# A GNN layer in f32 on one core: where the first batch's residual is loaded

## The chip, the cores and the metric

The kernel runs on one core of a Trainium2 chip. The metric is the device time of one execution in microseconds (us). Before the change the median of three runs is 2159.79 us (2157.69 to 2161.91).

## What is computed

One layer of a gated graph network over 32 graphs (called batches here) of 512 nodes with 256 features, all in float32. The reference, cut to what matters:

```python
h = relu(layernorm(x))                                   # (32, 512, 256)
xc = transpose(h)                                        # channels first
c = relu(bn1(conv1d(xc, conv1_w)))                       # 1 tap
c = bn2(conv1d(c, conv2_w, pad=8))                       # 17 taps
x_conv = transpose(relu(c + xc))
s = h @ w_se.T + b_se                                    # 3 features
A = exp(-squared_distances(s)) * adj                     # (512, 512) for each batch
x_nmp = A @ relu(h @ w_msg.T + b_msg)
gi = concat([x_conv, x_nmp]) @ w_ih.T + b_ih             # 512 -> 3*256
gh = h @ w_hh.T + b_hh                                   # 256 -> 3*256
r = sigmoid(gi_r + gh_r); z = sigmoid(gi_z + gh_z)
n = tanh(gi_n + r * gh_n)
out = x + (1 - z) * n + z * h                            # the last "x +" is the residual
```

## The kernel before

Everything is kept with features on the 128 partitions and the 512 nodes of a batch along the free dimension; 256 features are two tiles, counted by `o` or `d`. The work runs as five streams: `rows` and `begins` (normalise, transpose, first convolution), `graphs` (messages, distances, the masked kernel and its product), `conv` (the 17 taps, as 25 products for each group of 4 batches, on transformed operands) and `gates` (the gated update, batch by batch).

**What sets the order.** The streams are Python generators. A planner written out in the kernel (the loop at L1106) keeps a clock of its own, `now`, advanced by an estimate for every matmul, and estimates of when VectorE (DVE) and ScalarE (ACT) are free. It always lets the stream go on that is furthest behind its share. So the order of each engine's instructions is settled when the program is built. A DMA issue moves none of these clocks: where a load stands in the program changes only the queue of the engine that issues it. Nearly all loads are issued by SyncE (SP), in program order; SP stands still at a load whose buffer is still being read, and all loads behind it wait too.

**The stretch around the change.** At the 25th product of the first group, `late_pools` (L686) opens the pool for the second half of the work and issues the gates' weights, `whh` (768 KB) and `wih` (1536 KB), on SP. This lets the stream `gates` begin: `all_gates` (L1058) waits for `late`, loads the residual of batch 0, and then runs `gates(b)` for each batch. `gates(b)` (L861) first loads `hTb` (512 KB, the normalised rows of its batch) and two tiles `xnb` (256 KB each, the graph's product), unless that was done ahead.

**The residual.** `load_res(b, o)` (L776) loads one half of a batch of `x` into a tile `res` of 128 x 512, of which the pool has three. `blocks` (L768) does it in four DMAs, one for each 32 rows. Each takes `x` in blocks of 32 x 32, laid out so that a later block transpose needs no other step; a piece that is contiguous in HBM is 32 floats, 128 B, so a DMA of 64 KB has 512 pieces. Batch 0's two halves are the eight DMAs of this case. For every later batch `store` issues the load of a half just when the half of the batch before has been stored (L928).

**Who reads it.** For each half `o`, `gates` sums four products in PSUM: `ps_r`, `ps_h`, `ps_z` and `ps_n`. Then `mix`, `mix_next`, `mix_last` and `leave` follow, each queued with `later` until the planner's clock has come to it. `leave` (L911) transposes the result block by block, adds it to `res` on DVE and queues `store`.

**The masks.** `Graphs.ask` (L253) loads 128 rows of the adjacency matrix into `m_sb` (256 KB, three buffers). Batches 0 to 7 take them row by row, and TensorE (PE) turns them with four transposes (L132, called from `masked`, L741); batches from 8 on take them in blocks of 32 x 32, in four DMAs. Each mask is asked for when the one three before it has been used.

Of the kernel before, what the change touches and what calls it, by code (L numbers as in the profile page):

```python
# [44 lines left out]
def kernel(  # L45
# [31 lines left out]
    ND = D // P  # L77
# [46 lines left out]
    def matmul(ps, lhsT, rhs, **more):  # L124
        nonlocal now
        now += max(0.22, elements(ps) / 600.0)
        nc.tensor.matmul(ps, lhsT, rhs, **more)  # L127
# [16 lines left out]
    def later(t, f):  # L144
        LATER.append((t, f))
        LATER.sort(key=lambda e: e[0])

    def settle():
        while LATER:
            LATER.pop(0)[1]()  # L150
# [29 lines left out]
    def load_gates(b):  # L180
        if b >= B or b in HB:
            return
        HB[b] = late.tile([P, ND, N], F32, name="hTb", bufs=2)
        nc.sync.dma_start(HB[b], HD[b])

    def load_sums(b, d):
        if b < B and (b, d) not in XN:
            XN[b, d] = late.tile([P, N], F32, name="xnb", bufs=2)
            nc.sync.dma_start(XN[b, d], ND_[b, d])
# [578 lines left out]
    def blocks(t, rows, o):  # L768
        for g in range(P // 32):
            at = o * P + 32 * g  # L770
            nc.sync.dma_start(
                t[32 * g : 32 * g + 32, :].rearrange("i (k j) -> i k j", j=32),
                rows[:, :, at : at + 32],
            )

    def load_res(b, o):  # L776
        if b < B and (b, o) not in XR:
            XR[b, o] = late.tile([P, N], F32, name="res", bufs=3)
            blocks(XR[b, o], XB[b], o)
# [81 lines left out]
    def gates(b):  # L861

        load_gates(b)
        load_sums(b, 0)
        load_sums(b, 1)
        hT = HB[b]
        parts = []
        x_in = []

        def cols(o, g):  # L870
            return slice(g * D + o * P, g * D + (o + 1) * P)

        def products(ps, o, g, first, last, of, then=None):


            sources = ((whh, 0), (wih, 0), (wih, ND))
            for k in range(first, last):
                w, at = sources[k]
                for i in range(ND):
                    matmul(  # L880
                        ps, w[:, at + i, cols(o, g)], hT[:, i, :] if k == 0 else x_in[2 * k - 2 + i],
                        start=(k == of[0] and i == 0), stop=(k == of[1] and i == ND - 1),
                    )
                if k == last - 1 and then is not None:
                    then()
                yield now

        def residual():
            xconv = XC.pop(b)[:, :, :N]
            dve.tensor_tensor(xconv, xconv, hT, op=ALU.add)  # L890
            yield dve.free + 0.3
            act.activation(xconv, xconv, AF.Relu)
            x_in.extend([xconv[:, i, :] for i in range(ND)] + [XN[b, d] for d in range(ND)])

        def mix_next(r, z, o, s):
            act.activation(
                r[:, s], r[:, s], AF.Tanh,
                bias=vec[:, _COL["b_ih"] + 2 * ND + o : _COL["b_ih"] + 2 * ND + o + 1],
            )
            later(act.free + 0.3, lambda: mix_last(r, z, o, s))  # L900

        def mix_last(r, z, o, s):
            if s.start == 0:
                parts.append(late.tile([P, N], F32, name="o_sb"))
            t = parts[-1]
            dve.tensor_tensor(t[:, s], hT[:, o, s], r[:, s], op=ALU.subtract)
            dve.tensor_tensor(t[:, s], z[:, s], t[:, s], op=ALU.mult)
            dve.tensor_tensor(r[:, s], r[:, s], t[:, s], op=ALU.add)
            later(dve.free, lambda: leave(r, t, o, s))

        def leave(r, t, o, s):  # L911

            dve.transpose(t[:, s], r[:, s])
            y = XR[b, o]
            dve.tensor_tensor(y[:, s], t[:, s], y[:, s], op=ALU.add)
            later(dve.free + 0.4, lambda: store(y, o, s))

        def store(y, o, s):
            for g in range(P // 32):
                at = slice(32 * g, 32 * g + 32)  # L920
                queue = nc.gpsimd if s.stop - s.start == N else nc.scalar if g % 2 else nc.sync
                queue.dma_start(  # L922
                    OB[b][:, s.start // 32 : s.stop // 32, o * P + 32 * g : o * P + 32 * g + 32],
                    y[at, s].rearrange("i (k j) -> i k j", j=32),
                )
            if s.stop == N:
                del XR[b, o]
                load_res(b + 1, o)  # L928

        for o in range(ND):  # L930
            r = z = None

            def reset():
                nonlocal r
                settle()
                r = late.tile([P, N], F32, name="r", bufs=2)
                act.activation(r, ps_r, AF.Sigmoid, bias=brz[:, o : o + 1])

            def reset_hidden():
                dve.scalar_tensor_tensor(  # L940
                    r, ps_h, vec[:, _COL["b_hh"] + 2 * ND + o : _COL["b_hh"] + 2 * ND + o + 1], r,
                    op0=ALU.add, op1=ALU.mult,
                )

            def update():
                nonlocal z
                z = late.tile([P, N], F32, name="z")
                act.activation(z, ps_z, AF.Sigmoid, bias=brz[:, ND + o : ND + o + 1])

            def mix(s=slice(0, N)):  # L950
                dve.tensor_tensor(r[:, s], ps_n[:, s], r[:, s], op=ALU.add)
                later(dve.free + 0.3, lambda r=r, z=z, o=o: mix_next(r, z, o, s))
                if o == ND - 1:
                    load_sums(b + 1, 0)
                    load_sums(b + 1, 1)

            ps_r = acc.tile([P, N], F32, name="ps_acc")
            if o == 0:
                yield lambda: b in evacuated
                yield evacuated[b]  # L960
                yield from residual()
                yield from products(ps_r, o, 0, 0, 1, (0, 2))
                yield act.free + LAG
            else:
                yield from products(ps_r, o, 0, 0, 1, (0, 2))
            yield from products(ps_r, o, 0, 1, 3, (0, 2), reset)
            ps_h = acc.tile([P, N], F32, name="ps_acc")
            yield from products(ps_h, o, 2, 0, 1, (0, 0), reset_hidden)
            ps_z = acc.tile([P, N], F32, name="ps_acc")
            yield from products(ps_z, o, 1, 0, 3, (0, 2), update)  # L970
            if o == 0:
                load_gates(b + 1)
            ps_n = acc.tile([P, N], F32, name="ps_acc")
            if b < B - 1 or o < ND - 1:
                yield from products(ps_n, o, 2, 1, 3, (1, 2), mix)
                continue

            for h in range(2):
                s = slice(h * N // 2, (h + 1) * N // 2)
                if h > 0:  # L980
                    ps_n = acc.tile([P, N], F32, name="ps_acc")
                for j in range(2 * ND):
                    matmul(
                        ps_n[:, s], wih[:, j, cols(o, 2)], x_in[j][:, s],
                        start=(j == 0), stop=(j == 2 * ND - 1),
                    )
                mix(s)
                yield now
            settle()
        gated.add(b)  # L990
# [66 lines left out]

    def all_gates():  # L1058
        yield lambda: late is not None
        for o in range(ND):  # L1060
            load_res(0, o)
        for b in range(B):
            yield from gates(b)

# [6 lines left out]
        "graphs": (all_graphs(), 49.0, 0.0),  # L1071
        "conv": (convolution(), 66.0, 0.0),
        "gates": (all_gates(), 125.0, 1.25),
    }
    clock = {name: at for name, (_, _, at) in streams.items()}
# [102 lines left out]
```

## Time and profile before

| What | us |
| --- | --- |
| median of three runs | 2159.79 |
| the profiled execution | 2163.09 |
| its span, first instruction to last | 2161.0 |
| PE busy in it | 2100.2 |
| DVE busy | 1523.7 |
| ACT busy | 763.7 |
| POOL (GpSimd) busy | 296.8 |

The span is what the profile's rows are measured in; the profiled execution has about 2 us around it. A few of its rows recur below. For the group `res<-in_x_dram` the list of DMA issues has 256 issues of 64 KB, with a median of 4.3 us from issue to landing. The masks stand there as 32 issues of 256 KB (3.6 us) and 384 of 64 KB (2.6 us), `hTb` as 32 issues of 512 KB (6.0 us). SP's queue, q1, moves 282.95 MB, and its packets take 48.3% of the 16 DMA engines' span.

How to read the lines: an instruction stands as line, engine, operation, `out<-in`, shape and count. In a timeline the first two numbers are start and duration, and square brackets hold how long the engine had been idle before it and what ended that. In a view of waits the three numbers are the total, how often, and the longest. L118, L127 and L132 are helpers that issue nearly all work of DVE and ACT, of matmuls and of transposes, so the tiles' names tell more than the line. PEld is PE's loading of weights, which overlaps its matmuls. An engine name with a q (SPq) is the engine's queue of issues.

### The profile page before, as it was taken

What the parts mean: (1) busy time and instruction counts of PE and PEld (TensorE: products, weight loads), DVE (VectorE), ACT (ScalarE), POOL (GpSimd) and SP (SyncE); (2) the same over time, 40 slices, a digit from 0 to 9 for tenths busy, and PEclk for the clock granted to TensorE, in tenths of its full rate; (3) what the DMA queues carried; (4) which work ended last, traced back from release to release, by engine and by line L of the source; (5) the groups of instructions that cost most, each with busy time, mean ns of one, the idle gap of its engine ahead of it and who ended that gap; (6) DMA issues with size and microseconds to landing.
All of it is one profiled execution on the core that took longest, in us unless ns stands there. A gap on an engine that the chain in (4) does not pass through costs nothing.

```text
span 2161.0 us, 26532 instructions
## 1 busy us (share of the span) xinstructions
PE 2100.2 (97%) x9200; PEld 1303.0 (60%) x9200; DVE 1523.7 (71%) x2818; ACT 763.7 (35%) x1277; POOL 296.8 (14%) x445
## 2 busy tenths in 40 slices
PE   7998899999999999999999999999999999999998
PEld 4876566566565666556665666556665566665443
DVE  6887588676777778668875777767777677776333
ACT  5635422424324342334424243243522325222311
POOL 1101112111111111111111111101111010011111
PEclk9999899999999999999999999999999999999999
DMA  7446566766666576756767656666676564554331
GB/s 269 164 156 217 169 195 176 235 173 181 169 201 176 168 194 183 206 165 173 191 181 212 184 160 194 189 174 189 180 183 161 151 161 138 142 169 90 71 73 34
DMA packets 539461, 367.11 MB, mean 170 GB/s; under 512 B 455232, under 2 KB 472000, under 8 KB 538688
## 3 DMA queue, kind: packets, MB, share of 16 engines
q1 hardware_dynamic: 511392, 282.95, 48.3%
q0 software_dynamic: 23248, 69.23, 10.1%
q10 hardware_dynamic: 4688, 13.24, 1.6%
q8 instruction: 73, 1.20, 0.2%
q14 instruction: 60, 0.49, 0.1%
HBM read 282.74 MB, written 82.58 MB: 169 GB/s over the span
## 4 chain that ended last, share of the span: by engine, by line
PE 83%; ACT 1%; DVE 1%; issue 0%; DVEq 0%; ACTq 0%
PE ps_acc L127 44%; PE ps_g L127 17%; PE ps_c L127 14%; PE ps_b L127 7%; PE ps_b L733 1%; PE ps_g L132 1%; ACT at L118 0%; DVE xconv L118 0%; ACT xconv L118 0%; ACT L118 0%; DVE r L118 0%; DVE o_sb L118 0%; PE ps_g L733 0%; DVE msg L118 0%; DVE res L118 0%
## 5 line engine op out<-in xcount | busy, mean ns | idle before, releaser
L127 PE MATMUL ps_acc<-xconv,wih 128*128 128x512 f32 (+1 forms) x772 | 362.5, 592 | 5.2 <-ACT xconv L118 5.2
L127 PE MATMUL ps_acc<-xnb,wih 128*128 128x512 f32 (+1 forms) x772 | 362.7, 592 | 0.0
L127 PE MATMUL ps_acc<-hTb,whh 128*128 128x512 f32 x768 | 355.6, 593 | 0.1
L127 PE MATMUL ps_c<-xd,w 128*128 128x116 f32 x2800 | 346.2, 277 | 4.4 <-DVE z L118 4.4
L127 PEld LDWEIGHTS ps_c<-xd,w 128*128 128x128 f32 x2800 | 332.0, 194 | 7.6 <-DVE z L118 4.8
L922 POOL DMA_DIRECT2D out_dram<-res x252 | 164.8, 660 | 942.3 <-DVE res L118 843.4
L118 DVE TENSOR_TENSOR r<-ps_acc,r 128x512 f32<-128x512 f32 (+1 forms) x65 | 44.4, 684 | 313.3 <-PE ps_acc L127 313.2
L127 PEld LDWEIGHTS ps_acc<-xnb,wih 128*128 128x128 f32 x772 | 141.9, 189 | 165.0 <-issue 163.4
L127 PEld LDWEIGHTS ps_acc<-xconv,wih 128*128 128x128 f32 x772 | 141.4, 190 | 157.2 <-issue 145.6
L127 PE MATMUL ps_g<-at,msg 128*128 128x512 f32 x512 | 229.5, 599 | 2.5 <-DVE at L118 2.5
L127 PEld LDWEIGHTS ps_acc<-hTb,whh 128*128 128x128 f32 x768 | 141.7, 190 | 148.1 <-issue 143.8
L127 PEld LDWEIGHTS ps_b<-x,w 128*128 128x128 f32 x1400 | 182.8, 192 | 71.1 <-issue 55.8
L118 ACT ACTIVATE mid<-ps_b 128x232 f32<-128x232 f32 x175 | 63.9, 365 | 370.7 <-PE ps_b L127 331.7
L127 PE MATMUL ps_b<-x,w 128*128 128x116 f32 x1400 | 184.3, 275 | 5.3 <-ACT at L118 5.3
L127 PEld LDWEIGHTS ps_g<-at,msg 128*128 128x128 f32 x512 | 97.1, 192 | 119.9 <-issue 113.7
L118 DVE SCALAR_TENSOR_TENSOR x<-x,x 128x480 f32<-128x480 f32 (+1 forms) x184 | 144.1, 783 | 3.0
L118 DVE TENSOR_TENSOR x<-x 128x240 f32<-128x240 f32 (+1 forms) x320 | 134.4, 462 | 0.5
L127 PE MATMUL ps_g<-wmsg,hTg 128*128 128x259 f32 x496 | 125.1, 384 | 0.7 <-ACT hT L118 0.7
L118 ACT ACTIVATE z<-ps_acc,brz 128x512 f32<-128x512 f32 x64 | 44.0, 687 | 220.5 <-PE ps_acc L127 220.3
L127 PE MATMUL ps_g<-hT,w 128*128 128x512 f32 x256 | 119.4, 610 | 1.2 <-ACT at L118 1.2
L127 PEld LDWEIGHTS ps_g<-wmsg,hTg 128*128 128x128 f32 x496 | 93.0, 191 | 44.4 <-issue 32.5
L118 DVE TENSOR_TENSOR xd<-x 128x480 f32<-128x480 f32 x175 | 113.2, 649 | 3.3 <-PE ps_c L127 3.3
(109 smaller groups left out, 2488.5 us busy)
## 6 DMA issues: line engine op xcount, KB each, us to landing
w<-wd SPq DMA_DIRECT2D x150, 768.0 KB, 5.8
m_sb<-in_adj_dram SPq DMA_DIRECT2D x384, 64.0 KB, 2.6
hd<-hT POOLq DMA_DIRECT2D x32, 512.0 KB, 5.7
res<-in_x_dram SPq DMA_DIRECT2D x256, 64.0 KB, 4.3
hTb<-hd SPq DMA_DIRECT2D x32, 512.0 KB, 6.0
xnb<-nd SPq DMA_DIRECT2D x64, 256.0 KB, 3.1
out_dram<-res POOLq DMA_DIRECT2D x252, 64.0 KB, 3.2
hTg<-hd SPq DMA_DIRECT2D x31, 512.0 KB, 4.4
```

Source lines behind the costliest of these rows:

```text
L118: getattr(self.engine, name)(*tiles, **more)
L127: nc.tensor.matmul(ps, lhsT, rhs, **more)
L132: nc.tensor.transpose(ps, a, ident)
L733: nc.tensor.matmul(pss[c], gr.left[k, :], gr.right[k, :], start=True, stop=True, tile_position=(32 * c, 0),)
L922: queue.dma_start(OB[b][:, s.start // 32 : s.stop // 32, o * P + 32 * g : o * P + 32 * g + 32], y[at, s].rearrange("i (k j) -> i k j", j=32),)
```

## The change

The eight loads of batch 0's residual are taken out of `all_gates`, where they stood ahead of `gates(0)` and so right behind the gates' weights. They now stand inside `gates(0)`, after the products into `ps_z` of the first half and behind the load of `hTb` for batch 1. Later batches are as before.

```diff
@@ gates(b), in the loop over the halves o
             yield from products(ps_z, o, 1, 0, 3, (0, 2), update)
             if o == 0:
                 load_gates(b + 1)
+                for k in range(ND if b == 0 else 0):
+                    load_res(0, k)
             ps_n = acc.tile([P, N], F32, name="ps_acc")
             if b < B - 1 or o < ND - 1:
                 yield from products(ps_n, o, 2, 1, 3, (1, 2), mix)
@@ all_gates()
         yield lambda: late is not None
-        for o in range(ND):
-            load_res(0, o)
         for b in range(B):
             yield from gates(b)
```

## The prediction

> **What bounds the kernel now.** I read the totals and slices first, then TensorE's waits, then the stretch that holds the longest of them. The page:
>
> ```profile
> span 2161.0 us, 26532 instructions
> PE 2100.2 (97%) x9200; PEld 1303.0 (60%) x9200; DVE 1523.7 (71%) x2818; ACT 763.7 (35%) x1277; POOL 296.8 (14%) x445
> ```
>
> TensorE (PE) is busy for 97% of the span. Its instructions run in one written order, so the time is its work plus its gaps, 60.8 us in all. The changed DMAs compute nothing, so they matter only through a gap. The view of waits for PE names the gaps:
>
> ```profile
> PE ps_g L132 <- DMA m_sb<-in_adj_dram: 13.5, 1, 13.5
> PE ps_g L132 <- ACT x_sb L118: 9.3, 1, 9.3
> PE ps_b L127 <- ACT at L118: 5.3, 6, 1.6
> ```
>
> The longest is one single wait of 13.5 us, for an adjacency mask from HBM. The second is the kernel's start. The timeline shows where the first lies, and SP's queue beside it:
>
> ```profile
> 204.52 0.33 SPq L470 DMA_DIRECT2D w<-wd  x1
> 204.90 10.41 SPq L771 DMA_DIRECT2D res<-in_x_dram  x8
> 215.36 0.49 SPq L184 DMA_DIRECT2D hTb<-hd  x1
> 215.94 0.85 SPq L189 DMA_DIRECT2D xnb<-nd  x2
> 216.88 0.38 SPq L173 DMA_DIRECT2D hT<-hd  x1
> 217.36 7.55 SPq L262 DMA_DIRECT2D m_sb<-in_adj_dram  x4
> ...
> 223.46 1.09 PE L132 MATMUL ps_g<-ident,m_sb 128*128 128x128 f32 x4 [13.50 <-DMA m_sb<-in_adj_dram]
> ```
>
> The eight `res` issues that the change moves stand right ahead of that mask: SP spends 10.41 us on them. The mask (the last of batch 3) is issued at 217.36 and lands 6.0 us later, at about 223.3; PE goes on at 223.46. Windows of that stretch tell what SP is held by (columns: time, busy us of PE, PEld, DVE, ACT, POOL, then the granted clock, DMA share, GB/s):
>
> ```profile
> 202.00:213.00 11.00, 7.47 (x44) 4.58 (x36) 6.84 (x8) 6.02 (x13) 0.00 (x0) 1.00 1.03 422
> 212.90:216.70 3.80, 0.00 (x0) 0.00 (x0) 2.66 (x3) 2.31 (x3) 0.00 (x0) 0.67 1.39 165
> 217.00:223.00 6.00, 0.00 (x0) 0.00 (x0) 0.00 (x0) 3.11 (x3) 0.00 (x0) 0.50 0.97 341
> ```
>
> The DMA engines are full from 202 to 223. First come the weights `whh` and `wih` (768 and 1536 KB) and three `w` at 422 GB/s, and SP's 10.41 us is mostly back pressure from them (one `res` issue took 4.83 us, the median one 0.49). From 212.9 to 216.7 the rate is 165 GB/s: there the profile counts 4256 packets, 4231 of them under 512 B, and the eight `res` loads are 8 x 512 = 4096 pieces of 128 B. So the mask waits for a backlog on the DMA engines, and not only for SP. That matters for the sum: the gain isn't 10.41.
>
> **The change, part by part.**
>
> *Removed from 204.90: eight DMAs.* In the shared backlog `res` holds 3.8 us. Without it `hTb` follows the weights at 212.9. Behind it come `xnb`, `xnb`, `hT` and the mask: 512 + 256 + 256 + 512 + 256 KB = 1.835 MB. SP reaches them early: issues of about 0.5 us from 204.9 put `hT` at 206.4. Its buffer was last read by the row product of 204.33, which ends at 207.94. The mask reuses a buffer that PE reads in the eight transposes from 207.78 to 208.82, so it is issued by about 209, well before 212.9. The wait for those bytes is then pure transfer. Before, they took from 216.7 to 223.3, 6.6 us, because SP fed them one at a time into emptying queues. At the 422 GB/s that the row shows for a backlog they take 4.35 us, with some 0.6 us to land about 4.95. So the gain is 3.8 us if they go no faster than before, and 3.8 + 1.65 = 5.45 us if they run at the backlog's rate. These are my two ends. I take 4.9, nearer to the second, since everything is queued before the engines get to it; 2 KB pieces (`xnb`, mask) are the reason not to take it all. The mask lands at about 218.4, and PE's wait is 8.6 us.
>
> The Trainium skill speaks against this size. "DMA: Bandwidth & Descriptors", section Specifications, puts the fabric ceiling at 435 GB/s, by which the 0.524 MB of `res` would be worth 1.2 us and the gain about 1.2 to 2.9. The same table says that pieces under 512 B fall short of line rate, and the row at 165 GB/s shows that here: 3.8 us measured decides.
>
> *The clock.* PE's granted clock falls about 4.2 us after PE stops (1.00 until 214.2) and comes back only at 231.2:
>
> ```profile
> 214.20:223.40 9.20, 0.00 (x0) 0.00 (x0) 1.36 (x3) 5.72 (x5) 0.00 (x0) 0.50 1.10 285
> 223.40:231.20 7.80, 6.96 (x11) 3.22 (x12) 1.82 (x2) 0.00 (x0) 0.00 (x0) 0.50 0.15 43
> ```
>
> A wait of 8.6 us still lets it fall, so the half clock after the restart (7.8 us, costing 3.9) stays. The shorter one that the page shows, after a 2.2 us wait at 298.6, held 3.4 us at half (mean 0.51 from 299.5 to 303). When the clock comes back may differ between executions by some 2.4 us of half clock: plus or minus 1.2 us; I take 0.
>
> *Does the gain last?* DVE, ACT and SP wait for PE after the restart: DVE sat idle 10.3 us before 236.7 and ACT 11.9 us before 232.05, and PE has no other wait for a DMA in the whole trace. The order on PE, DVE, ACT and POOL stays as it is, since the planner's clock doesn't count DMA issues. So all shifts together; I carry the full 4.9.
>
> *Added after `load_gates(1)`: the same eight DMAs.* In the old times, `hTb` for batch 1 is issued at 269.39, and SP's next instruction starts 7 us later:
>
> ```profile
> 268.99 0.37 SPq L262 DMA_DIRECT2D m_sb<-in_adj_dram  x1
> 269.39 0.43 SPq L184 DMA_DIRECT2D hTb<-hd  x1
> 276.81 3.00 SPq L470 DMA_DIRECT2D w<-wd  x2
> ...
> 280.56 0.69 DVE L118 TENSOR_TENSOR res<-o_sb,res 128x512 f32<-128x512 f32 x1
> ```
>
> Eight issues at 0.49 are 3.9 us, 269.8 to 273.7: they fit ahead of the 276.81 with 3.1 us left. The packets come after `hTb`, which landed at 275.3 (5.9 us). The first four loads are 1.9 us of packets, so they land at about 277.8; the add that reads them runs at 280.56: 2.8 us of cover. The other four land at about 279.7 and are read at 332.16. The moved packets may hold up the `w` of 276.81 by up to 3.8 us, from 280.1 to 283.9; the sum that reads it is the `w` group at 287.17 by my count. POOL only stores the result of the add. I cost this part at 0, with a low bound of 0 (nothing is removed here). The high bound takes the first `res` loads' longest landing, 10.0 us: the fourth, issued near 271.3, would land at 281.3, 0.8 us late. If the cover goes, DVE stands at the add, and `xd`, the mask's product `at` and `n` behind it (281.17 to 282.34) are late for PE, microsecond for microsecond.
>
> **The sum.** -4.9 + 0 + 0 = -4.9 us: the span goes from 2161.0 to 2156.1. The profiled execution took 2163.09, 3.3 above the median of the runs, 2159.79; the forecast is 2159.8 - 4.9 = **2154.9 us**, from 2153.1 to 2157.3 with the clock's 1.2 us on each side of 3.8 and 5.45.
>
> **Rivals.**
>
> *The mask is hardly earlier (2158.6).* The bytes count and not the pieces: 0.524 MB at 422 GB/s is 1.2 us. Or SP is still held, by `hT`'s buffer for one. For it: SP's issues were held by the full queues, and these stay full until 212.9. Against it: 4231 small packets in 3.8 us with almost nothing else moving.
>
> *Slower: `res` comes late to the add at 280.56.* For it: DVE runs in order, TensorE's next products wait for it, and the cover is 2.8 us after a stretch in which stores of `w` and `hTb` share the engines. The gap is paid in full and costs 1.7 more when the clock halves for 3.4 us, as at 299.5. It eats the gain when the loads land 3.2 us late, at 283.8. With 8 us it gives 8 + 1.7 - 4.9 = +4.8: 2164.6. Against it: that is a landing 17 us after its issue, where the longest seen, in the worst backlog, is 10.0.
>
> *The wait goes altogether (2142.4).* If the mask overtook the weights there would be no 13.5 us and no half clock: -17.4. Against it: one queue in order, full until 212.9. The change not doing what it says is excluded: issue order on SP is the order in the program, and no load of `res` remains early.
>
> **How the numbers follow.** Forecast 0.78, hardly earlier 0.12, late `res` 0.08, wait gone 0.02. About 0.2%, 4.3 us, is what a measurement can tell. The forecast's own range crosses that bound (2155.5): I give 0.60 of its 0.78 to the side below it, as 4.9 lies above 4.3. Faster is 0.60 + 0.02 = 0.62, same 0.18 + 0.12 = 0.30, slower 0.08. The range is 2151.5 to 2159.0: the first case with the 2 us or so that the runs scatter, and most of the second.
>
> **What would show it.** In the changed profile the mask's wait is 8 to 9.5 us, `res` is gone from the stretch before it and the DMA rate there stays above 300 GB/s; `res` is issued right after the second `hTb`, and the add doesn't wait for a DMA. A wait of over 11 us refutes the backlog's arithmetic, a DVE wait for `res` the cover, and a new PE gap after 230 the claim that the gain lasts.

## The result, and the profile after

The changed kernel is faster, and by more than what its runs scatter. The first comparison gave 2153.61 us (median of 4 runs, 2152.67 to 2154.48) against 2159.96 us, a ratio of 0.9971 with a 95% interval of 0.9954 to 0.9988. With more runs of both it is 2154.11 us against 2160.77 us, ratio 0.9971, interval 0.9961 to 0.9981: 6.3 us less, between 4.1 and 8.4. The forecast was 2154.9 us.

The waits of TensorE in the changed kernel (total, times, longest), with the kernel's start now ahead of the mask:

```profile
PE ps_g L132 <- ACT x_sb L118: 9.2, 1, 9.2
PE ps_g L132 <- DMA m_sb<-in_adj_dram: 8.6, 1, 8.6
```

The mask's wait went from 13.5 to 8.6 us, as forecast. SP's queue in the same stretch, and PE's restart:

```profile
200.85 0.49 SPq L693 DMA_DIRECT2D wih<-in_w_ih_dram  x1
203.27 0.33 SPq L470 DMA_DIRECT2D w<-wd  x1
203.65 0.42 SPq L184 DMA_DIRECT2D hTb<-hd  x1
204.16 0.86 SPq L189 DMA_DIRECT2D xnb<-nd  x2
205.11 0.38 SPq L173 DMA_DIRECT2D hT<-hd  x1
207.15 11.61 SPq L262 DMA_DIRECT2D m_sb<-in_adj_dram  x4
...
217.31 1.08 PE L132 MATMUL ps_g<-ident,m_sb 128*128 128x128 f32 x4 [8.61 <-DMA m_sb<-in_adj_dram]
```

The first mask is issued at 207.15, 10.2 us earlier than before, but it takes 10.0 us to land and not 6.0: the engines are still busy with the weights. The windows show that they now stay busy right through (time, busy us of PE, PEld, DVE, ACT, POOL, granted clock, DMA share, GB/s):

```profile
201.00:211.30 10.30, 7.21 (x40) 4.58 (x36) 6.41 (x7) 6.02 (x13) 0.00 (x0) 0.94 1.03 426
211.30:217.20 5.90, 0.00 (x0) 0.00 (x0) 2.99 (x4) 4.07 (x4) 0.00 (x0) 0.50 1.03 397
217.30:223.70 6.40, 5.60 (x10) 2.63 (x11) 1.82 (x2) 1.56 (x2) 0.00 (x0) 0.50 0.23 66
```

There is no stretch at 165 GB/s any more. The half clock after the restart lasts 6.3 us here, where it was 7.8.

The eight loads in their new place (SP), and the add that needs the first four (DVE):

```profile
262.79 0.43 SPq L184 DMA_DIRECT2D hTb<-hd  x1
263.26 8.44 SPq L771 DMA_DIRECT2D res<-in_x_dram  x8
271.87 1.09 SPq L470 DMA_DIRECT2D w<-wd  x2
...
273.69 0.69 DVE L118 TENSOR_TENSOR res<-o_sb,res 128x512 f32<-128x512 f32 x1
```

No bracket stands behind the add: it didn't wait. The fourth load was issued at 265.29 and took 6.7 us, so it landed at 272.0, with 1.7 us of cover.

**Why the two profiled spans differ by more.** They are 2161.0 and 2150.6 us, 10.4 apart. The distance between like instructions in the two traces grows in steps. It is 1.3 us already at the transposes before the wait (209.30 and 208.04), where the change has not acted yet. The wait adds 4.9, which makes 6.15 at the restart. The earlier return of the clock adds 0.7 by the next common wait (298.64 and 291.77). Two steps of 1.6 us follow, and there the clocks differ, here after the wait for `z` near 333, before and after:

```profile
333.60:337.10 3.50, 3.50 (x18) 3.50 (x19) 0.35 (x1) 1.56 (x2) 2.16 (x4) 0.51 0.72 157
```

```profile
326.50:330.00 3.50, 3.50 (x23) 2.81 (x24) 1.42 (x4) 1.62 (x2) 2.30 (x5) 1.00 0.65 131
```

After the same kind of wait (2.2 and 2.1 us) TensorE ran at half clock for 3.4 us in the one execution and at full clock in the other. The second step is such a stretch at 746.6 that has no match at 737.9. But a second profile of the changed kernel has it (738.7, clock 0.50). So 4.9 of the 10.4 us are the wait, and the rest is how long and how often the clock was halved, which differs between executions of one and the same program.

### The profile page after: what moved, and what is told of

Read it like the earlier page. It is cut to its first block, busy times and chain, and to the rows that moved or that the text cites. A ratio compares the mean times of both kernels' runs of the same rounds, so it can differ in the third digit from the quotient of the medians.

```text
span 2150.6 us, 26534 instructions
## 1 busy us (share of the span) xinstructions
PE 2092.6 (97%) x9200; PEld 1297.0 (60%) x9200; DVE 1522.8 (71%) x2818; ACT 762.9 (35%) x1277; POOL 295.9 (14%) x445
## 3 DMA queue, kind: packets, MB, share of 16 engines
q0 software_dynamic: 23248, 69.23, 10.2%
## 4 chain that ended last, share of the span: by engine, by line
PE 83%; ACT 1%; DVE 1%; issue 0%; DVEq 0%; ACTq 0%
PE ps_acc L127 44%; PE ps_g L127 17%; PE ps_c L127 13%; PE ps_b L127 7%; PE ps_b L733 1%; PE ps_g L132 1%; ACT at L118 0%; DVE xconv L118 0%; ACT xconv L118 0%; ACT L118 0%; DVE r L118 0%; DVE o_sb L118 0%; PE ps_g L733 0%; DVE msg L118 0%; DVE res L118 0%
```

## The experiments

In two profiles each, the mask's wait was 13.5 and 13.9 us in the kernel before, 8.6 and 9.3 us in the changed one. So two profiles of one kernel lie 0.4 and 0.7 us apart; a smaller difference says nothing. The question is what of those eight DMAs delays the mask: SP's time, the pieces, the bytes or their number.

**Half of them back.**

```diff
         yield lambda: late is not None
+        load_res(0, 0)
```

> The changed kernel, with the first half of batch 0's residual (four of the eight loads) back in the old place. In the changed kernel TensorE waits 8.6 us for the last mask of batch 3, in the kernel before 13.5 us. If the pieces of res take time on the DMA engines in line ahead of the mask, half of them put back half: about 1.9 us of packets and some refilling, a wait of 10.5 to 11.1 us. If SP's issue time is what counts, the wait follows SP: the first four issues took 6.4 of the 10.4 us, so 8.6 + 4.9 x 0.61 = 11.6 us. The two lie close; the run is mainly a check that the effect comes in doses.

The wait was 11.6 us: the effect comes in doses. It falls on the number that went by SP's time, but the 11.1 of the pieces lies within the scatter. SP's queue in that run:

```profile
203.23 6.48 SPq L771 DMA_DIRECT2D res<-in_x_dram  x4
209.75 2.35 SPq L184 DMA_DIRECT2D hTb<-hd  x1
```

The four issues alone took 6.48 us (the third 4.95), and in SP's waits of the stretch none of them, nor `hTb`, waits for a landing. So `hTb` was issued at 209.75, where the changed kernel issues it at 203.65. The number alone, by the rule found below, would have let `hTb` go by 205.4, but the mask itself not before 213.1; it went at 213.62.

**Issued by another queue.**

```diff
-            blocks(XR[b, o], XB[b], o)
+            blocks(XR[b, o], XB[b], o, nc.gpsimd if b == 0 else nc.sync)
```

> The kernel before, with the eight loads of batch 0's residual in the old place but issued by GpSimd's queue and not by SP's. Theory (work on the shared DMA engines): SP is free early, but the same 4096 pieces still run on the same engines before the mask, and the wait stays at 12 to 13.5 us. Rival (SP's queue held by the issues): SP goes straight on to hTb and the mask, and the wait falls to 8.6 us as in the changed kernel.

The wait grew to 16.2 us. SP was as free as in the changed kernel (queue of that run):

```profile
202.22 0.33 SPq L470 DMA_DIRECT2D w<-wd  x1
202.60 0.43 SPq L184 DMA_DIRECT2D hTb<-hd  x1
203.12 1.16 SPq L189 DMA_DIRECT2D xnb<-nd  x2
204.37 0.46 SPq L173 DMA_DIRECT2D hT<-hd  x1
206.10 10.94 SPq L262 DMA_DIRECT2D m_sb<-in_adj_dram  x3
```

and the shared engines had become slower, 238 GB/s where the changed kernel had 426 and then 397 (a window of that run):

```profile
206.00:218.00 12.00, 1.16 (x9) 0.69 (x7) 7.21 (x8) 6.66 (x8) 1.56 (x3) 0.62 1.02 238
```

16.2 us is above both numbers that were expected. So freeing SP while the same rows run beside the weights doesn't help, and SP's time can't be all. It is no clean price for the pieces, though: on GpSimd's queue the profile counts 261 packets for these 0.54 MB, not some 4096, so they go out in another form there.

**Large pieces, eight DMAs.** Batch 0's residual is read in another layout, so its output differs.

```diff
+            if b == 0:
+                rows = x[0].rearrange("(p k) d -> p (k d)", k=NT)
+                for g in range(P // 32):
+                    at = slice(32 * g, 32 * g + 32)
+                    nc.sync.dma_start(XR[b, o][at, :], rows[at, o * N : (o + 1) * N])
+                return
             blocks(XR[b, o], XB[b], o)
```

> The kernel before, but the eight early loads of batch 0's residual take rows of x in contiguous pieces of 2 KB (256 pieces for the same 512 KB, still eight DMAs of 64 KB at the old place); what is added to batch 0 is then not its residual. Theory (number of pieces): 0.52 MB in large pieces run at some 400 GB/s, 1.3 us, so the wait is 8.6 + 1.3 = 9.9 us. Rival (bytes or the number of DMAs, whatever the pieces): 13.5 us as before.

The wait was 12.8 us. Sixteen times fewer pieces saved about 1 us, not 3.6. SP was held in another way now, by its waits in the stretch:

```profile
SPq L783 <- DMA wih<-in_w_ih_dram: 3.4, 1, 3.4
...
SPq L783 <- DMA w<-wd: 1.8, 2, 1.4
SPq L783 <- DMA whh<-in_w_hh_dram: 1.6, 1, 1.6
```

Each of the last four issues (L783) stood until an earlier DMA had landed: the seventh was issued at 210.41, when `wih` had landed at 210.40, the eighth at 212.10, when `w` had at 212.09. That led to the next two runs.

**Large pieces, two DMAs.** Against the run before:

```diff
-                for g in range(P // 32):
-                    at = slice(32 * g, 32 * g + 32)
-                    nc.sync.dma_start(XR[b, o][at, :], rows[at, o * N : (o + 1) * N])
+                nc.sync.dma_start(XR[b, o], rows[:, o * N : (o + 1) * N])
```

> As the run with 2 KB pieces, but the same 512 KB in two DMAs and not eight; again what is added to batch 0 is not its residual. With eight DMAs of 2 KB pieces the mask's wait was 12.85 us, hardly less than with 128 B pieces. Theory now: SP may have only so many DMAs out (each of the last five of those eight was issued in the moment when an earlier DMA landed), so eight small ones keep hTb from being queued behind the weights and the engines run dry; with two DMAs there is no such hold, and the wait is 8.6 us and the 1.3 us of the bytes, 9.9 us. Rival (the bytes themselves, whatever their number): 12.85 us again.

The wait was 10.8 us: 2.1 less with the same bytes in the same pieces. That is above the 9.9 expected from the changed kernel's 8.6; from its other profile, 9.3, it would be 10.6.

**Eight DMAs with nearly nothing in them.**

```diff
         yield lambda: late is not None
+        for k in range(ND):
+            XR[0, k] = late.tile([P, N], F32, name="res", bufs=3)
+            for g in range(P // 32):
+                part = slice(32 * g, 32 * g + 32)
+                nc.sync.dma_start(XR[0, k][part, :32], XB[0][:, 0, k * P + 32 * g : k * P + 32 * g + 32])
```

In `gates` the real loads go into the same tiles (`blocks` in place of `load_res`).

> The changed kernel, with eight more loads at the old place, each of only 4 KB (32 pieces of 128 B) into the later residual tiles; the real loads follow at the new place. They bring nearly no bytes and 256 pieces in all. If the count of DMAs holds SP (an issue waits until the DMA eight before it has landed), the eighth is issued only when the w of about 203 has landed, hTb follows it at about 212.5 into empty engines, and the mask's wait is 11.5 to 12.5 us. If bytes or pieces are what counts, it is 8.6 to 9.5 us as in the changed kernel.

The wait was 13.3 us, more than the 11.5 to 12.5 expected: 32 KB in place of 512 KB bring back the whole delay. The wait views of that run, first SP's in the stretch, then PE's:

```profile
SPq L1066 <- DMA wih<-in_w_ih_dram: 3.4, 1, 3.4
SPq L1066 <- DMA w<-wd: 2.2, 3, 1.0
...
SPq L1066 <- DMA whh<-in_w_hh_dram: 1.6, 1, 1.6
```

```profile
PE ps_g L132 <- DMA m_sb<-in_adj_dram: 13.3, 1, 13.3
```

The small loads (L1066) wait for `w`, `whh`, `wih` and `w`, with which they share no data. In the trace the completions of SP's loads go round on eight semaphores, and an issue waits until the DMA eight before it on this queue has landed: the seventh is issued at 210.27, `wih` had landed at 210.26. In its queue the eighth is issued when that `w` (201.41, 10.2 us to landing) is there, and `hTb` right after:

```profile
201.41 0.33 SPq L470 DMA_DIRECT2D w<-wd  x1
201.79 10.13 SPq L1066 DMA_DIRECT2D res<-in_x_dram  x8
211.96 0.42 SPq L184 DMA_DIRECT2D hTb<-hd  x1
```

By then the engines have run dry (windows of the same run):

```profile
201.00:210.00 9.00, 5.35 (x24) 2.91 (x22) 6.96 (x8) 4.45 (x10) 0.00 (x0) 1.00 1.02 422
210.00:213.00 3.00, 0.00 (x0) 0.00 (x0) 2.44 (x3) 1.72 (x2) 0.00 (x0) 0.67 0.11 21
213.00:219.90 6.90, 0.00 (x0) 0.00 (x0) 0.00 (x0) 4.00 (x4) 0.00 (x0) 0.50 0.92 321
```

From 210 to 213 they move 21 GB/s. So the number alone is enough for the delay, without bytes and nearly without pieces.

It doesn't follow that the number is what held SP in the kernel before. All its waits from 200 to 220 in that kernel:

```profile
SPq L470 <- PE ps_c L127: 1.9, 1, 1.9
SPq L470 <- ACT x_sb L118: 0.6, 1, 0.6
```

No `res` issue (L771) waits for a landing there. The eight follow one another at once, and it is the issues that are long: the third takes 4.83 us, where with 2 KB pieces it took 0.41. The eighth starts at 214.82; by the number alone it could have started at 214.48, when `w` had landed. Both holds end within half a microsecond of each other, and the engines move the 4096 pieces in the time for which they stand nearly empty in this run. Which of the two the kernel before pays for can't be told apart. Whether the 4096 pieces would delay the mask as much in one or two DMAs, no run shows.

**Loaded early, but behind the masks.**

```diff
             gr.ask(1)
+            if (b, c) == (3, 2):
+                load_res(0, 0)
+                load_res(0, 1)
```

This stands in `masked`; the loads in `gates` are taken out.

> The changed kernel, with batch 0's residual issued some 50 us earlier than there, but behind the three masks and not ahead of hTb. If it matters only that these eight DMAs are not ahead of the mask, the wait is 8.6 to 9.4 us as in the changed kernel, and the add has some 50 us of cover. If the stretch as a whole is too full for them, wherever they stand in it, the wait is above 10 us.

The wait was 9.7 us and the one time 2154.51 us. It lies between the two numbers expected, slightly above the two profiles of the changed kernel and far from 13.5. What counts is that the eight are not ahead of the mask, not that they come 50 us later.

**Is the load covered in its new place?** The first try moved the two calls into `mix`, a few products on.

> The changed kernel, with batch 0's residual loaded still later: after the products into ps_n of the first half, two products of four matmul calls and other work behind the new place. The cover of the load is tested. In the changed kernel the first four loads land at 272.0 and the add runs at about 273.7, 1.7 us of cover. Issued some 5 us later, they land some 3 to 6 us after the add could run: DVE waits 2 to 5 us for a DMA, and TensorE shows a new or longer wait for DVE near 275 to 290 of up to the same length. Rival (the load is covered wherever it stands in these gates): no DVE wait for res and no new TensorE wait.

It tested nothing: no other load is issued in between, so SP's order was the same, and DVE showed no wait for `res`. The second try put them into `leave`, ahead of `dve.transpose`:

```diff
+            if b == 0 and o == 0:
+                load_res(0, 0)
+                load_res(0, 1)
             dve.transpose(t[:, s], r[:, s])
```

> The changed kernel, with batch 0's residual issued behind the next load of w, directly ahead of the transpose and the add that need it. (The run that put it some products later left SP's order as it was, since no other issue stood between, so it didn't test the cover.) SP issues that w when its buffer is free, at about 270 us; the first four res then land at about 274.5 to 276, where the add could run at about 273.7. If the cover is thin as forecast, DVE waits 1 to 3 us for the DMA of res, and TensorE waits longer for DVE between 274 and 295. If there is slack behind DVE, TensorE's waits stay as they are (one of 2.2 us near 291).

DVE waited 3.0 us for it, and PE got one new wait:

```profile
276.10 0.69 DVE L118 TENSOR_TENSOR res<-o_sb,res 128x512 f32<-128x512 f32 x1 [2.98 <-DMA res<-in_x_dram]
```

```profile
PE ps_c L127 <- DVE z L118: 2.2, 1, 2.2
PE ps_g L127 <- DVE at L118: 1.1, 1, 1.1
```

Of 3.0 us on DVE 1.1 reached TensorE. The run's one time, 2151.98 us, lies within the changed kernel's scatter (2151.67 to 2156.21).

**What holds the mask for the other 8.6 us?** Two versions take more from ahead of it. The first issues the weights behind the third of batch 3's masks, and not in `late_pools`:

```diff
@@ late_pools()
-        nc.sync.dma_start(whh, w_hh)
-        nc.sync.dma_start(wih, w_ih)
@@ masked(b, at, c)
             gr.ask(1)
+            if (b, c) == (3, 2):
+                nc.sync.dma_start(whh, w_hh)
+                nc.sync.dma_start(wih, w_ih)
```

> The changed kernel, with the gates' weights whh and wih (2304 KB) issued only after the third mask of batch 3 has been used, so behind the mask that TensorE waits for. Theory (the wait that is left is the weights' time on the DMA engines): the mask has only three w, hTb, xnb and hT ahead of it and lands at about 210.5; the wait falls from 8.6 us to some 2 us, the clock doesn't fall to half there (13.7 us at half in the changed kernel, some 4 us of it lost in work), and TensorE reads the weights some 15 us later, when they have long landed: about 10 us faster than the changed kernel, near 2143 us. Rival (something else holds the mask, or the weights come late to the first gates): the wait stays above 6 us, or a new wait of several us for wih or whh stands ahead of the first ps_acc.

The time fell to 2152.31 us (2148.91 to 2152.57; ratio to the kernel before 0.9959, 0.9944 to 0.9973), where about 2143 was expected, and the wait to 4.4 us only:

```profile
PE ps_g L132 <- DVE y L118: 4.4, 1, 4.4
```

The view names DVE, but the mask landed at 212.68 and PE went on at 212.82, the same 0.14 us behind the landing as in the kernel before. The expectation doesn't list two transfers that ran ahead of the mask as well, a load `x_sb` and a store `hd` of 512 KB each. At 422 GB/s they are 2.5 us by estimate, and the mask landed 2.2 us later than the 210.5 expected. The clock halved all the same, and stayed there for some 8 us after the restart. The second moves `load_gates(0)` and both `load_sums(0, d)` there too, ahead of the weights:

```diff
             if (b, c) == (3, 2):
+                load_gates(0)
+                load_sums(0, 0)
+                load_sums(0, 1)
                 nc.sync.dma_start(whh, w_hh)
@@ gates(b)
+        if b == 0:
+            yield lambda: 0 in HB
         load_gates(b)
```

> The changed kernel, with hTb, the two xnb and then the weights whh and wih of the first gates all issued behind the third mask of batch 3's four, so that the mask TensorE waits for has only the w and the row load hT ahead of it. Theory (the wait is the time of what stands ahead on the DMA engines): the 1 MB of hTb and xnb less than in the run with the weights alone moved is 2.5 us; the wait falls from 4.4 to about 2 us, the clock no longer halves there or only for 3.4 us, and the kernel is 8 to 10 us faster than the changed one, near 2144 to 2146 us, if nothing new waits for hTb or the weights. Rival (the rest of the wait isn't the DMA's): 4.4 us stays, near 2151 us.

2150.52 us (2146.64 to 2152.2), ratio 0.9949 (0.9935 to 0.9962): the lowest median of all, 10.2 us below the kernel before and 3.6 below the changed one, where 8 to 10 were expected. From the run with the weights alone moved it isn't told apart, as the intervals overlap. The mask landed at 208.99 here. The timeline shows what took its place:

```profile
206.45 3.13 DVE L118 TENSOR_TENSOR y<-y,z 128x1392 f32<-128x1392 f32 x2
...
209.50 0.68 DVE L118 TENSOR_TENSOR at<-ps_g,at 128x512 f32<-128x512 f32 x1
...
210.24 0.66 PE L132 MATMUL ps_g<-ident,m_sb 128*128 128x128 f32 x4 [2.94 <-DVE at L118]
...
211.61 1.88 DVE L118 TENSOR_TENSOR at<-ps_g,at 128x512 f32<-128x512 f32 x3
...
213.55 5.11 PE L127 MATMUL ps_g<-at,msg 128*128 128x512 f32 x6 [2.65 <-DVE at L118]
```

TensorE now waits twice for DVE, 2.9 and 2.7 us: the products with the mask stand behind the convolution's sums `y` in DVE's order. A faster mask alone can't win that back. The clock was at half from 211.3 to 218.2 here too.

The run of the changed kernel for comparison, and that of the kernel before:

> The changed kernel itself, for a time beside the other kernels of this call. The profile so far gave 4.9 us by the shorter mask wait; the medians 6.35 us. If 4.9 us is the lasting effect and the rest is where the half-clock stretches fell, the difference of the medians over more runs lies between 4.5 and 6.5 us. If more than the mask wait got shorter, it stays above 6.5 us.

2154.11 us against 2160.77: 6.66 us between the medians, just above the upper of the two bounds. The wait was 9.3 us in its profile; that more than the wait got shorter isn't shown, since the interval reaches from 4.1 to 8.4 us.

> The kernel before once more, for the scatter of its profile. The mask's wait of TensorE was 13.5 us in the first profile; the changed kernel's was 8.6 and 9.3 us in two. If the wait is set by what stands ahead of the mask, it is 13 to 14.2 us again. The half-clock stretch at it lasted 17.1 us; it ends on a beat of 3.4 us, so 13.7 to 20.5 us can be had here without any change.

The wait was 13.9 us and the half clock 17.1 us again.

## Why the prediction was right, point by point

- **The place and the size.** TensorE's wait for the mask was forecast at 8.6 us and is 8.6 and 9.3. The term of 4.9 us for it holds: the profiles show 4.2 to 5.3. The 1.835 MB from `hTb` to the mask took 4.6 us behind the landing of `w`, where 4.95 were reckoned at the backlog's rate.
- **What the first term misses:** "In the shared backlog `res` holds 3.8 us." The engines did run these pieces for 3.8 us, and that stretch is gone in the changed kernel. But by this reading eight DMAs with hardly any pieces or bytes would cost nothing, and eight of 64 KB in 2 KB pieces 1.3 us. They brought the wait to 13.3 and 12.8 us, two with the same bytes to 10.8. What the sum had left out is the number: eight issues are one whole turn of SP's eight completion semaphores, so `hTb` and all behind it can't be issued before the `w` behind the weights has landed. In the kernel before, that hold ends at 214.5, and the long issues end at about the same time. That the price of the pieces came out as the price of the eight is therefore luck.
- **The second part of the term, 1.65 us for refilling,** fits either cause: in both, SP issues `hTb` and the rest only after the eight. They ran at 341 GB/s so, and at 397 in the changed kernel.
- **"SP's 10.41 us is mostly back pressure".** The trace bears it out: no issue waits for a landing, and single ones are stretched to 4.83 us. But without that SP would have stood almost as long, until the last `w` landed (204.52 + 10.0 = 214.5; the eighth `res` was issued at 214.8). The rival that SP is still held, "by `hT`'s buffer for one", did not come true: `hT` was issued at 205.11.
- **The page's figure.** By the fabric ceiling of 435 GB/s in the Trainium skill ("DMA: Bandwidth & Descriptors", Specifications) the forecast put the bytes at 1.2 us. The rows at 422 and 426 GB/s stay below that ceiling. In two DMAs of 2 KB pieces the bytes cost 1.5 to 2.2 us over the changed kernel's wait, near that estimate and far from 4.9.
- **The clock, costed at 0 with 1.2 us on each side.** It came back 6.3 and 5.5 us after the restart, where it had been 7.8; the forecast gives no working for its 2.4 us, and these three differ by 2.3. It fell 1.3 and 4.6 us after PE stopped, not always 4.2. These differences, and short stretches of half clock elsewhere, are the likely source of the difference between 4.9 and the 6.3 us of the medians. Only the wait's part is shown.
- **The gain lasts.** No new wait of TensorE stands behind the stretch, and later instructions keep the distance.
- **The cover.** Forecast 2.8 us, it was 1.7: SP needed 8.44 us for the eight issues, and not 3.9 (two of them took 2.4 us each), and the next `w` was issued 1.7 us late, which TensorE didn't wait for. "Microsecond for microsecond" was too dear: 1.1 of 3.0 us reached TensorE when the cover was taken away.
- **A sum.** The upper end of 3.8 and the clock's 1.2 us is 2157.2, not 2157.3.

## What to carry to other kernels

Count the DMAs ahead of an urgent load on its queue, not only their bytes: here eight small ones used up all that could be in flight, and whatever stood behind them was issued only when the large transfers had landed. Look at the length of the issues too, which held SP by themselves in the run with four. When SP waits for a DMA that shares no data with its next load, look how many issues lie between the two. Place loads by the order within their queue; moving the residual in the program past other engines' work, with no other issue between, changed nothing here.

## What the runs showed of the hardware

The same loads from a second queue slowed the transfers beside them: with the eight issued by GpSimd the engines moved 238 GB/s where the changed kernel's moved 426 and 397, and the mask came later than with all on one queue (16.2 us of wait against 13.5). And the clock of TensorE halved for 3.4 us after a wait of 2.2 us in some executions and not in others of the same length (0.51 and 1.00 above).
